# Two layernormed attention blocks on one Trainium2 core: inverse square roots as clamp and power on GpSimd, and a new order of the stages

## The chip, the cores and the metric

The kernel runs on one core of one Trainium2 chip. The metric is device time in microseconds for one execution; lower is better. The engines are named as the profile names them: PE (TensorE's matmuls), PEld (its weight loads), DVE (VectorE), ACT (ScalarE), POOL (GpSimd) and SP (SyncE, which issues most transfers).

## The reference

Eight sequences of 1024 tokens with 256 features pass first through a causal single-head attention with a residual and a layernorm (the first stage), then through a two-layer local transformer with 8 heads of 64 and a window of 128, then through a residual and a last layernorm. One local layer is, cut to what matters here:

```python
h = shift_token(x)                       # second half of the features moved by one token
q, k, v = split(h @ wqkv)
q = l2norm(q) * qs; k = l2norm(k) * ksc  # q / clip(||q||, 1e-12), head by head
q, k = rotary_xpos(q, k)
o = local_attention(q, k, v)             # each window of 128 sees itself and the one before
x = x + o @ wo
h = shift_token(x)
h = (h - mean(h)) / sqrt(var(h) + 1e-05) * lg + lb
a, g = split(h @ w1 + b1)
x = x + (a * gelu(g)) @ w2 + b2
```

Inverse square roots occur in three places: in `l2norm` (of the sum of squares of each head), in the layernorm ahead of the feed-forward part, and in the two outer layernorms.

## The kernel before, in words

The first stage (`fronts`) handles the eight sequences one after the other and writes its result to DRAM. Then `layers` walks over 2 layers x 8 sequences x 8 windows of 128 tokens, in 64 pairs of windows. Matrix products are done in split form: an operand is cut into a rounded high part and a remainder, and three products are added up.

The work on a window is cut into named stages. `prep` loads and transposes x for a pair. `qk` (twice a window, `k` 0 and 1) projects queries and keys of four heads (`l_pqk`), squares them on ACT (L705), sums the squares on DVE into `l_ss` (L708), multiplies the projections with the rotary tables on DVE (L715) and adds the two halves on POOL (L722). `unit` turns the sums of squares of a window, 16 numbers per token, into inverse norms `l_nrm` through `rsqrt`, and scales the keys with them on POOL (L733); the queries' norms are applied later, by the mask pass on the scores (L793). `turn` transposes queries and keys on PE (`l_t`, L756) and splits them into a ring of three windows. `sc` makes the scores of four heads, masks them on DVE (L793) and takes the exponential on ACT (`l_e`); `et` transposes the result (L832), `v` projects the values, `val` multiplies (`l_po`, L849), `out` divides by the denominators (L858, L863, L864), and `proj` projects back (`l_py`).

When the odd window of a pair is projected, the feed-forward part of the pair is put on a queue. It is a generator with eleven steps; the item `side` in the order runs the next step. The first step moves rows by one token with small transfers, takes mean and variance on DVE, calls `rsqrt` for 2 numbers per token (`m_rs`) and normalizes (`m_hn`, L917). The second transposes (`m_hp`) and splits. Six steps make the wide product and the gelu (`m_pag`, L965 to L970, whose last part on POOL is `m_a`), two the product back (`m_pf`), and the last adds the residual; in the second layer it also does the last layernorm, with an `rsqrt` of its own (`o_rs`). The first stage has a layernorm too (`f_rs`, 4 numbers per token, 16 calls).

The order of the stages is written out by hand in `ORDER`. For every pair `j` the list is run through once; an item `("sc", -2, 0)` means the scores of the heads' first half for window `2j - 2`. The instructions are written in that order, and the scheduler of the tile framework may move one ahead of another on its engine where its own model of the engines finds the earlier one not ready, so that the order on a chip is near the list, not the list itself. Each engine then takes its instructions in the order given. PSUM has four banks for the general tiles (`ps`) and four for scores (`sc`).

In `rsqrt`, the value is clamped or offset and scaled, its bits are read as an integer to make a first guess, and two refining steps follow: nine DVE instructions (L112 to L129).

Of the kernel before, what the change touches and what calls it, by code (L numbers as in the profile page):

```python
# [8 lines left out]

FP = mybir.dt.float32  # L10
FR = mybir.dt.float32r
I32 = mybir.dt.int32
AF = mybir.ActivationFunctionType
ALU = mybir.AluOpType
AX = mybir.AxisListType

P = 128
# [4 lines left out]
EPS = 1e-5  # L22
FAR = 1e30
BIG = 3e38
RS = (1595890143.0, 2.371616, -6.578563, 19.474865, 212.91114082351987)


@with_exitstack
def kernel(
# [31 lines left out]
    nc = tc.nc  # L61
# [22 lines left out]
    const = ctx.enter_context(tc.tile_pool(name="const", bufs=1))  # L84
# [20 lines left out]

    def rsqrt(sm, src, n, low, op, name):

        k, c1, c2, c3, f = RS  # L110
        a = sm([P, n], f"ra{n}", f"{name}_a", bufs=2)
        nc.vector.tensor_scalar(a, src, low, f, op, ALU.mult)  # L112
        seed = sm([P, n], f"ri{n}", f"{name}_i", bufs=2, dt=I32)
        nc.vector.tensor_scalar(seed, a.bitcast(I32), -0.5, k, ALU.mult, ALU.add)
        y = seed.bitcast(FP)
        t = sm([P, n], f"rt{n}", f"{name}_t", bufs=2)
        nc.vector.tensor_tensor(t, a, y, ALU.mult)
        u = sm([P, n], f"ru{n}", f"{name}_u", bufs=2)
        nc.vector.scalar_tensor_tensor(u, t, -1.0, y, ALU.mult, ALU.mult)
        z = sm([P, n], f"rz{n}", f"{name}_z", bufs=2)  # L120
        nc.vector.scalar_tensor_tensor(z, u, c1, y, ALU.add, ALU.mult)
        t = sm([P, n], f"rt{n}", f"{name}_t2", bufs=2)
        nc.vector.tensor_tensor(t, a, z, ALU.mult)
        h = sm([P, n], f"ru{n}", f"{name}_h", bufs=2)
        nc.vector.tensor_tensor(h, t, z, ALU.mult)  # L125
        p = sm([P, n], f"rp{n}", f"{name}_p", bufs=2)
        nc.vector.scalar_tensor_tensor(p, h, c2, h, ALU.add, ALU.mult)  # L127
        r = sm([P, n], f"ry{n}", f"{name}_y", bufs=6)
        nc.vector.scalar_tensor_tensor(r, p, c3, z, ALU.add, ALU.mult)  # L129
        return r  # L130

    def mean_rstd(sm, parts, mv, i, name):
# [7 lines left out]
    def rstd_of(sm, mv, n, name):  # L140
        return rsqrt(sm, mv[:, :, 1], n, EPS, ALU.add, name)


    ident = const.tile([P, P], FP, name="ident")
    make_identity(nc, ident)
    identr = const.tile([P, P], FR, name="identr")
# [5 lines left out]
    for j, s in ((0, 1), (1, -1), (2, 1)):  # L152
        nc.gpsimd.affine_select(
            out=mask[:, j, :], in_=mask[:, j, :], compare_op=ALU.is_ge, fill=FAR,
# [339 lines left out]
    def load_ffn(l, stage, ps, W):  # L494
# [90 lines left out]
    QB = 4  # L585
    PSB = {"ps": 4, "sc": 4}
    ORDER = [
        ("side", 1), ("out", -4), ("side", 1), ("side", 1), ("unit", -1), ("proj", -4),
        ("unit", -2), ("turn", -2, 0), ("turn", -1, 0), ("turn", -1, 1), ("sc", -2, 0),
        ("turn", -2, 1), ("qk", 0, 0), ("out", -3), ("side", 1), ("sc", -2, 1), ("side", 1),  # L590
        ("side", 1), ("proj", -3), ("sc", -1, 0), ("qk", 0, 1), ("v", 1), ("et", -2, 0),
        ("sc", -1, 1), ("et", -2, 1), ("v", 0), ("et", -1, 0), ("val", -2, 0), ("et", -1, 1),
        ("prep", 2), ("qk", 1, 0), ("side", 1), ("side", 1), ("qk", 1, 1), ("val", -1, 0),
        ("val", -2, 1), ("val", -1, 1), ("side", 1), ("side", 1), ("side", 1),
    ]

    def layers(pool, psum):
# [59 lines left out]
        def attention(l, b, W, finished):  # L657
# [67 lines left out]
            def unit(t):  # L725

                n = f"l{l}_{b}_{t}"
                nrm = rsqrt(sm, st.pop(("ss", t)), 2 * HEADS, 1e-24, ALU.max, f"{n}_nrm")
                st["nrm", t] = nrm
                n4 = nrm.rearrange("p (g k h) -> p g k h", g=2, k=2)  # L730
                for k in range(2):
                    kk = st["r", t, k][:, INNER // 2 :].rearrange("p (h d) -> p h d", d=DH)
                    nc.gpsimd.tensor_tensor(  # L733
                        kk, kk, n4[:, k, 1, :].unsqueeze(2).to_broadcast([P, HEADS // 2, DH]),
                        ALU.mult,
                    )
# [311 lines left out]
    with tc.tile_pool(name="fpool", bufs=1) as fpool, tc.tile_pool(  # L1048
        name="fpsum", bufs=1, space=PSUM
    ) as fpsum:  # L1050
        fronts(fpool, fpsum)
    with tc.tile_pool(name="lpool", bufs=1) as lpool, tc.tile_pool(
        name="lpsum", bufs=1, space=PSUM
# [59 lines left out]
```

## Time and profile before

| | us |
|---|---|
| median of three runs | 2795.12 |
| lowest and highest | 2794.61, 2795.77 |
| the profiled execution's own time | 2790.89 |
| its span, first to last instruction | 2789.1 |

The granted TensorE clock was 0.984 of full speed over the span. The page gives the busy time of each engine; groups of instructions by line, with busy time, mean duration and the idle time of the engine ahead of them; the chain that ended last, followed back from the last instruction to whatever released each step; and waits. PE's ends are modelled, so its busy share says that it has work in flight, not that it runs at its peak. Durations below come from the profiled execution.

### The profile page before, as it was taken

The page shows a single profiled execution, that of the slowest core. Times are in us where ns is not written, and L with a number is a line of the kernel's source. Part 1 is how long each engine was busy: PE and PEld are TensorE (multiplying, and loading weights), DVE is VectorE, ACT ScalarE, POOL GpSimd, SP SyncE. Part 2 cuts the span into 40 slices and gives each one's busy share as a digit, 9 for nine tenths or more (in the row PEclk, how much of TensorE's full clock was granted, in tenths as well). Part 3 has the DMA queues.
Part 4 walks back from the last instruction along what each step waited for, and adds up shares of the span by engine and source line. Part 5 has one row for each costly group of instructions (what it writes and reads, how often), then busy time and mean ns, then how long its engine had stood idle before and what let it go on. Part 6 is the DMA issues. An engine that isn't in the chain of part 4 may idle for free.

```text
span 2789.1 us, 63147 instructions
## 1 busy us (share of the span) xinstructions
PE 2703.2 (97%) x22336; PEld 2350.4 (84%) x22336; DVE 2440.2 (87%) x8464; ACT 1748.8 (63%) x4486; POOL 1245.9 (45%) x1515
## 2 busy tenths in 40 slices
PE   7998999999999999999999999999999999999997
PEld 5776688888888888888888788888888888888886
DVE  6887789888889988889888899999999999999995
ACT  6675566666666666666666566666666666666663
POOL 4553244444444444344453444444444454444442
PEclk9999899999999999999999999999999999999998
DMA  6332011011111111111111111111111111111110
GB/s 181 97 98 86 26 39 43 28 43 43 43 41 39 34 38 43 43 41 39 37 57 52 57 51 49 39 41 49 51 50 40 39 48 50 51 41 43 43 47 24
DMA packets 146126, 139.83 MB, mean 50 GB/s; under 512 B 28680, under 2 KB 122768, under 8 KB 145808
## 3 DMA queue, kind: packets, MB, share of 16 engines
q1 hardware_dynamic: 144448, 135.32, 16.0%
q8 instruction: 176, 2.88, 0.4%
q14 instruction: 142, 1.16, 0.1%
q10 hardware_dynamic: 1360, 0.46, 0.1%
HBM read 95.35 MB, written 27.81 MB: 44 GB/s over the span
## 4 chain that ended last, share of the span: by engine, by line
PE 69%; DVE 22%; ACT 3%; DMA 3%; issue 2%; POOL 0%; SPq 0%; DVEq 0%; POOLq 0%; ACTq 0%
PE l_pqk L104 11%; PE m_pag L104 9%; PE m_pf L104 9%; PE l_sc L785 8%; PE l_et L832 7%; PE l_po L849 6%; PE l_pv L104 5%; PE l_py L104 4%; PE l_t L756 3%; DVE l_t L715 3%; DVE m_gl L966 3%; DVE m_a L969 2%; DVE l_nrm_p L127 1%; DVE l_ss L708 1%; DVE l_sc L793 1%
## 5 line engine op out<-in xcount | busy, mean ns | idle before, releaser
L722 POOL TENSOR_TENSOR l_t<-l_t,l_t 128x256 f32<-128x256 f32 x512 | 367.5, 739 | 855.1 <-DVE l_t L715 816.0
L654 ACT ACTIVATE l_e<-l_sc,l_nm 128x256 f32<-128x256 f32 (+1 forms) x992 | 450.6, 462 | 288.4 <-DVE l_nm L793 279.3
L104 PE MATMUL m_pag<-m_hT,w_h 128*128 128x256 f32 (+1 forms) x2816 | 515.1, 285 | 6.4 <-DVE l_t L715 3.3
L793 DVE CUSTOM_DVE_ANT_0 l_sc<-l_sc,mask,l_nrm_y 128x256 f32<-128x256 f32 (+1 forms) x1024 | 453.6, 470 | 50.6 <-ACT l_e L654 36.0
L104 PEld LDWEIGHTS m_pag<-m_hT,w_h 128*128 128x128 f32 (+1 forms) x2816 | 430.3, 187 | 21.1 <-issue 10.5
L654 ACT ACTIVATE m_gl<-m_pag,b 128x256 f32<-128x256 f32 (+1 forms) x384 | 181.4, 474 | 385.2 <-PE m_pag L104 332.6
L104 PE MATMUL m_pag<-m_hT,w_l 128*128 128x256 f32 (+1 forms) x1408 | 393.7, 280 | 0.0
L104 PE MATMUL l_pqk<-wqk_h,l_xT 128*128 128x512 f32 x1024 | 392.4, 424 | 0.8 <-ACT l_xT L92 0.8
L715 DVE TENSOR_TENSOR l_t<-l_pqk,l_tab 128x512 f32<-128x512 f32 x512 | 329.8, 680 | 0.0
L835 ACT COPY l_eT<-l_et 128x512 f32<-128x512 f32 (+1 forms) x512 | 276.0, 567 | 80.6 <-PE l_et L832 56.3
L970 POOL TENSOR_TENSOR m_a<-m_gl,m_a 128x256 fp32r<-128x256 f32 x320 | 241.4, 762 | 113.2 <-DVE l_nrm_h L125 55.4
L832 PE MATMUL l_et<-ident,l_e 128*128 128x128 f32 x1920 | 269.9, 279 | 4.4 <-ACT l_eT L835 3.4
L104 PEld LDWEIGHTS m_pag<-m_hT,w_l 128*128 128x128 f32 (+1 forms) x1408 | 264.7, 188 | 0.0
L832 PEld LDWEIGHTS l_et<-ident,l_e 128*128 128x128 f32 x1920 | 215.2, 141 | 49.9 <-ACT l_eT L835 13.3
L104 PE MATMUL m_pf<-w_h,m_a 128*128 128x256 f32 x1280 | 249.5, 284 | 0.0
L849 PE MATMUL l_po<-l_eT,l_v 128*64 128x128 f32 x3840 | 242.0, 278 | 0.7 <-ACT l_eT L835 0.6
L104 PEld LDWEIGHTS l_pqk<-wqk_h,l_xT 128*128 128x128 f32 x1024 | 196.0, 191 | 53.9 <-ACT l_xT L92 1.2
L849 PEld LDWEIGHTS l_po<-l_eT,l_v 128*64 128x64 f32 x3840 | 209.5, 138 | 35.2 <-issue 18.8
L104 PEld LDWEIGHTS m_pf<-w_h,m_a 128*128 128x128 f32 x1280 | 203.5, 188 | 11.0 <-POOL m_a L970 0.2
L864 POOL TENSOR_TENSOR l_oT<-l_on,l_oT 128x512 fp32r<-128x512 f32 x128 | 165.0, 1289 | 97.5 <-ACT l_oT L863 92.6
L785 PE MATMUL l_sc<-ring,ring 64*128 64x256 f32 (+1 forms) x2048 | 207.5, 283 | 0.0
L104 PE MATMUL l_py<-wo_h,l_oT 128*128 128x256 f32 x1024 | 205.0, 282 | 0.0
(195 smaller groups left out, 6636.4 us busy)
## 6 DMA issues: line engine op xcount, KB each, us to landing
l_R<-rd_d SPq DMA_DIRECT2D x256, 128.0 KB
x<-x_d SPq DMA_DIRECT2D x96, 256.0 KB
l_tab<-tab_d SPq DMA_DIRECT2D x128, 128.0 KB
xin<-in_L_attn_x_dram SPq DMA_DIRECT2D x16, 512.0 KB
x_d<-xin SPq DMA_DIRECT2D x16, 512.0 KB
rd_d<-l_rT SPq DMA_DIRECT2D x512, 1.0 KB
x_d<-x SPq DMA_DIRECT2D x32, 256.0 KB
out_dram<-x SPq DMA_DIRECT2D x32, 256.0 KB
```

Source lines behind the costliest of these rows:

```text
L104: nc.tensor.matmul(dst, a, b, start=(i == 0), stop=(i == len(steps) - 1))
L654: ins = nc.scalar.activation(*args, **kw)
L715: nc.vector.tensor_tensor(tt[j].rearrange("p (k h d) -> p k h d", k=2, d=DH), p3, tb.unsqueeze(2).to_broadcast([P, 2, HEADS // 2, DH]), AL ...
L722: nc.gpsimd.tensor_add(a[:, :, s, :], a[:, :, s, :], bsw[:, :, 1 - s, :])
L756: nc.tensor.transpose(pt[:, cols], r[:, cols], ident)
L785: nc.tensor.matmul(sc[i][:, j, 0:nk], ring[x][rows, 0, c, slot, :], ring[y][rows, 1, c, keys, :], start=(m == 0), stop=(m == 2),)
L793: nc.vector.tensor_tensor_reduce(dst, dst, mk, st["nrm", w][:, 8 * u + h : 8 * u + h + 1], BIG, ALU.add, ALU.min, nm[:, one],)
L832: nc.tensor.transpose(pt[:, a, i, :], e[:, i, j, a * P : (a + 1) * P], ident)
L835: nc.scalar.copy(eT[:, j, 0:m], pt[:, 0:m])
L849: nc.tensor.matmul(po[i * DH : (i + 1) * DH, c * P : (c + 1) * P], st["v", t][:, head * DH : (head + 1) * DH], eT[:, j, a, i, :], start=(a ...
L864: nc.gpsimd.tensor_tensor(oT[1], on, oT[0].bitcast(FP), ALU.subtract)
L970: nc.gpsimd.tensor_tensor(a[1], gl[0:z, :], a[0].bitcast(FP), ALU.subtract)
```

## The change

Two edits are made together. `rsqrt` becomes two GpSimd instructions: clamp (or offset), then a power with a constant tile of -0.5, in place of the nine DVE instructions. And `ORDER` is replaced by another order of the same items: `unit` of the even window comes ahead of that of the odd one and farther from it, the turns are set apart by other work, the transposes of the scores of window -2 are done together, and the value products lie elsewhere. Buffers and everything else stay.

```diff
-RS = (1595890143.0, 2.371616, -6.578563, 19.474865, 212.91114082351987)
...
     def rsqrt(sm, src, n, low, op, name):
-        k, c1, c2, c3, f = RS
         a = sm([P, n], f"ra{n}", f"{name}_a", bufs=2)
-        nc.vector.tensor_scalar(a, src, low, f, op, ALU.mult)
-        seed = sm([P, n], f"ri{n}", f"{name}_i", bufs=2, dt=I32)
-        nc.vector.tensor_scalar(seed, a.bitcast(I32), -0.5, k, ALU.mult, ALU.add)
-        y = seed.bitcast(FP)
-        t = sm([P, n], f"rt{n}", f"{name}_t", bufs=2)
-        nc.vector.tensor_tensor(t, a, y, ALU.mult)
-        u = sm([P, n], f"ru{n}", f"{name}_u", bufs=2)
-        nc.vector.scalar_tensor_tensor(u, t, -1.0, y, ALU.mult, ALU.mult)
-        z = sm([P, n], f"rz{n}", f"{name}_z", bufs=2)
-        nc.vector.scalar_tensor_tensor(z, u, c1, y, ALU.add, ALU.mult)
-        t = sm([P, n], f"rt{n}", f"{name}_t2", bufs=2)
-        nc.vector.tensor_tensor(t, a, z, ALU.mult)
-        h = sm([P, n], f"ru{n}", f"{name}_h", bufs=2)
-        nc.vector.tensor_tensor(h, t, z, ALU.mult)
-        p = sm([P, n], f"rp{n}", f"{name}_p", bufs=2)
-        nc.vector.scalar_tensor_tensor(p, h, c2, h, ALU.add, ALU.mult)
+        nc.gpsimd.tensor_scalar(a, src, low, None, op)
         r = sm([P, n], f"ry{n}", f"{name}_y", bufs=6)
-        nc.vector.scalar_tensor_tensor(r, p, c3, z, ALU.add, ALU.mult)
+        nc.gpsimd.tensor_tensor(r, a, half.to_broadcast([P, n]), ALU.pow)
         return r
...
+    half = const.tile([P, 1], FP, name="half")
+    nc.gpsimd.memset(half, -0.5)
...
     ORDER = [
-        ("side", 1), ("out", -4), ("side", 1), ("side", 1), ("unit", -1), ("proj", -4),
-        ("unit", -2), ("turn", -2, 0), ("turn", -1, 0), ("turn", -1, 1), ("sc", -2, 0),
-        ("turn", -2, 1), ("qk", 0, 0), ("out", -3), ("side", 1), ("sc", -2, 1), ("side", 1),
-        ("side", 1), ("proj", -3), ("sc", -1, 0), ("qk", 0, 1), ("v", 1), ("et", -2, 0),
-        ("sc", -1, 1), ("et", -2, 1), ("v", 0), ("et", -1, 0), ("val", -2, 0), ("et", -1, 1),
-        ("prep", 2), ("qk", 1, 0), ("side", 1), ("side", 1), ("qk", 1, 1), ("val", -1, 0),
-        ("val", -2, 1), ("val", -1, 1), ("side", 1), ("side", 1), ("side", 1),
+        ("side", 1), ("unit", -2), ("out", -4), ("side", 1), ("proj", -4), ("turn", -2, 0),
+        ("unit", -1), ("turn", -2, 1), ("side", 1), ("turn", -1, 0), ("sc", -2, 0),
+        ("turn", -1, 1), ("sc", -2, 1), ("side", 1), ("qk", 0, 0), ("side", 1), ("out", -3),
+        ("qk", 0, 1), ("side", 1), ("proj", -3), ("sc", -1, 0), ("et", -2, 1), ("et", -2, 0),
+        ("v", 1), ("side", 1), ("v", 0), ("et", -1, 0), ("val", -2, 0), ("prep", 2),
+        ("sc", -1, 1), ("side", 1), ("qk", 1, 0), ("et", -1, 1), ("val", -2, 1), ("qk", 1, 1),
+        ("val", -1, 0), ("val", -1, 1), ("side", 1), ("side", 1), ("side", 1),
     ]
```

More of the change, by code (lines that the diff above doesn't have):

```diff
@@ L11 @@
 FR = mybir.dt.float32r
-I32 = mybir.dt.int32
 AF = mybir.ActivationFunctionType
```

## The prediction

> **What bounds the kernel now.** I read the page first: which engine is full, and whether it is full everywhere.
>
> ```profile
> PE 2703.2 (97%) x22336; PEld 2350.4 (84%) x22336; DVE 2440.2 (87%) x8464; ACT 1748.8 (63%) x4486; POOL 1245.9 (45%) x1515
> ```
>
> TensorE's bar is full, but its ends are modelled, so I went to the chain that ended last, through one pair of windows of layer 0, from one group of `l_xp` transposes to the next.
>
> ```profile
> 908.32 0.44 PE l_xp L677 x4
> 908.75 1.53 PE l_pqk L104 x6
> 910.28 0.44 PE m_hp L931 x4
> 910.72 1.39 PE l_pqk L104 x6
> 912.10 1.90 PE l_po L849 x32
> 914.00 8.01 PE m_pag L104 x66
> 922.01 1.43 PE l_py L104 x12
> 923.44 2.01 PE l_t L756 x16
> 925.45 1.11 PE l_sc L785 x12
> ...
> 945.53 1.02 PE l_et L832 x8
> 946.56 0.48 PE l_xp L677 x4
> ```
>
> Columns: start, length, what. All of it is TensorE, each run beginning where the last ended: 946.56 - 908.32 = 38.24 us a pair, 64 pairs, some 2400 us of the 2789.1. Six score matmuls and the like run at their own pace; only `l_t`, 2.01 us for 16 transposes where four of `l_xp` take 0.44 (16 would take 1.76), shows waiting. So the vector work that the change removes lies beside TensorE here. Is that so in layer 1? Two stretches of four pairs (one sequence), the first of layer 0, the second of layer 1, side by side in the table by windows; the columns are PE, PEld, DVE, ACT, POOL busy.
>
> ```profile
> 412.20:563.50 151.30, 151.15 (x1287) 133.72 (x1286) 134.57 (x449) 97.74 (x248) 66.24 (x86) 1.00 0.13 40
> 1685.00:1839.30 154.30, 153.11 (x1291) 134.64 (x1290) 142.32 (x510) 98.05 (x248) 71.30 (x89) 1.00 0.15 46
> ```
>
> TensorE issues the same matmuls, yet layer 1 takes 3.0 us more, with DVE at 142.32 of 154.30. The chain inside that second stretch tells why:
>
> ```profile
> 1783.70 0.74 DVE l_nrm_u L119
> 1784.64 0.40 DVE m_gl L966
> 1785.58 0.68 DVE l_nrm_p L127
> ...
> 1788.22 0.67 DVE l_nrm_y L129
> 1788.88 0.41 DVE m_gl L966
> ...
> 1790.89 0.66 PE l_t L756 x4
> ```
>
> Here the pieces of `rsqrt` stand between TensorE's runs: DVE sets the end for some 9 us in one pair of four. That is where the change can pay.
>
> **The removed instructions.** Nine on DVE for each call, 240 calls: 128 in `unit` on 16 columns, 64 + 32 on 2, 16 on 4. In the groups by shape the nine `l_nrm` rows are busy 73.2 + 51.0 + 45.6 + 41.0 + 29.9 + 26.1 + 23.9 + 23.3 + 22.4 = 336 us (2.6 us a call), the nine `m_rs` rows 92, `o_rs` 65, `f_rs` some 25: 518 us, 21% of DVE. Some of it is waiting:
>
> ```profile
> L127 DVE SCALAR_TENSOR_TENSOR l_nrm_p<-l_nrm_h x128: 161/660/733, 280.4 to 2713.3; 128x16 f32<-128x16 f32 x128
> ```
>
> Minimum, median and maximum in ns: 161 when free, mostly as long as one GpSimd operation (606 to 735 ns median). The Trainium skill, "GPSIMD Engine Reference", section 8, says that the two engines share SBUF interfaces and collide where the vector instruction has two SBUF inputs; by it about 9 x 0.16 = 1.5 us of a call is work and the rest waiting, and both end alike.
>
> Priced on the path, not by the 518 us: (a) layer 0 and 1, each pair: the waits in `l_t` go, 2.01 - 1.76 = 0.25 us. (b) layer 1's excess, 3.0 us x 8 sequences = 24 us: I take two thirds, -16, since score and transpose runs are also cut finer there, which the change need not mend. (c) between the layers (1450 to 1460, 1490 to 1502, 1533 to 1541) and near 2710 the same `l_nrm` pieces are on the chain: four places at 2 us, -8. Bounds for (b) and (c): 0 and -24, 0 and -15. In the first stage 16 calls of nine pieces at some 0.17 us lie among 260 us that wait on many things: within 3 us either way, taken as nothing.
>
> **The added instructions.** A clamp and a power on GpSimd. No row shows a power. Below: GpSimd's plain products cost 739 ns for 256 columns and 1289 for 512, so 2.15 ns a column and 0.19 us fixed; 16 columns make 0.22 us, and that is the clamp. Above: the nine-piece DVE chain, 2.7 us, as another iterated way to the same function. I take 2.0 us (nine GpSimd passes of 0.22 us), nearer the upper end because the work is alike; 2 columns, 0.5 us. The same skill page, section 7, charges a dependent fp32 chain 4 cycles an element at 1.2 GHz; a chain of 30 steps would be an estimated 1.6 us for 16 columns, and the sum would not move.
>
> Where does it lie? Per pair GpSimd is busy 17.95 of 38.24 us; 2 x 2.2 + 0.7 (0.7 more in layer 1) makes some 23. The tight stretch runs from the second `l_pqk` of a pair to the first `m_pf`, in the new order 1.90 (values) + 7.28 (60 of the 66 `m_pag`) + 1.43 + 0.88 + 0.73 + 0.44 + 0.91 + 0.44 + 0.91 = 14.9 us. `l_ss` is there 2.0 us in (912.10 to 914.14 in the timeline), so 12.9 us are left, and in them stand
>
> ```profile
> L722 POOL TENSOR_TENSOR l_t<-l_t,l_t 128x256 f32<-128x256 f32 x512 | 367.5, 739 | 855.1 <-DVE l_t L715 816.0
> L970 POOL TENSOR_TENSOR m_a<-m_gl,m_a 128x256 fp32r<-128x256 f32 x320 | 241.4, 762 | 113.2 <-DVE l_nrm_h L125 55.4
> L864 POOL TENSOR_TENSOR l_oT<-l_on,l_oT 128x512 fp32r<-128x512 f32 x128 | 165.0, 1289 | 97.5 <-ACT l_oT L863 92.6
> ```
>
> 2 x 0.74 + 6 x 0.76 + 1.29 and four of L733 at 0.65 = 9.9 us: 3.0 us left. One unit's 2.2 us fits; the other's sums of squares are ready half a pair earlier, where GpSimd idles over 3 us at a time (816.0 us in all, the first row's last column). Cost on the path: nothing, while clamp and power stay under 3.0 us and the first unit is early. The new wait is GpSimd's for `l_ss`; queued behind it are L722, L970 and L864, and TensorE waits for those in `l_t`, `m_pf`, `l_py`. DVE's mask pass L793 and `m_hn` now wait for GpSimd.
>
> **The new order.** Eleven feed-forward steps a pair as before, exps and gelus alternate twice a pair as before. By runs of TensorE: the turns stand apart (saving counted in a); a value run of 32 (1.90) becomes 16 and 16 (1.05 each in the layer 1 chain) and the transposes behind such a run take 1.02 for 0.87: +0.35; 16 `l_et` together, -0.15; two fewer `l_pqk` runs straight behind scores (1.59 for 1.39), two transposes there instead: -0.1; a split `m_pag` +0.1. With (a) about -0.1 a pair (bounds -0.35 to +0.3): -6 us over 64.
>
> From `l_py` of the odd window to `m_hp` there are now 8.9 us of TensorE runs (12 before). The timeline has 10.1 us from that `l_py`'s end (934.67) to the last `m_hn` (944.72), of which `rsqrt` is 940.39 to 943.56: 6.9 us are left and 0.7 of GpSimd, so 1.3 us spare if GpSimd is free, as it is there (3.3 us idle before L921). SP's transfers move with their stages (shifted rows with the first feed-forward step, reciprocals with the scores, x with `prep`); the table loads have no producer to wait for, so I price that at nothing; if it is uncovered, a landing of some 3 us in a pair would show. For small new waits I put 0.1 us a pair, +6.
>
> **Sum.** -6 - 16 - 8 + 6 = -24 us on the profiled execution's 2790.9 (span 2789.1 and 1.8 around it): 2767. The median of the three runs, 2795.1, is 4.2 above it: 2771.
>
> **Rivals.** (1) No change: TensorE is full, DVE was covered, the new order gives back what layer 1 gains. For it: layer 0's chain. Against: the layer 1 chain. 2795 within 5. (2) Slower: the power is dear. From 3.0 us for clamp and power (or if both units fall in the tight stretch) every further us delays `m_pf` or `l_t` each pair; at 4.25 us 1.25 x 64 = 80, less 24: 2851. Against: GpSimd's half-empty pair. For: its 3 us of room there. (3) Slower: 16 `l_et` fill four PSUM banks just behind the scores, ACT (24.73 us of 38.24, dense there) runs four exps at 0.68 us (475 + 203 ns) before it can empty the second bank, and `l_pv` waits up to 1.3 us. Above 0.4 us a pair it outweighs the gain; at the full 1.3, 83 less 24: 2854. Against: before, ACT was as dense and TensorE did not wait. (4) The order alone undone by more runs, +0.3 a pair: +19 - 24, same as (1).
>
> **Chances.** Forecast 0.48; no change (1, 4) 0.10; (2) 0.20; (3) 0.22. A difference of 0.2%, 5.6 us, is about what a measurement of this kernel can tell. Low end: (a) to (c) at their gaining bounds, -0.35 x 64 - 24 - 15 = -61, not all at once: 2742. High end: near the full price of (2) or (3), 2850; dearer cases are left out. The forecast's own range is 2742 to 2789.
>
> **What would show it.** Right: DVE near 1920 us; layer 1's four pairs under 152 us; no `l_nrm` piece on the chain; `l_t` waiting on nothing long; clamp and power under 3 us. Wrong: POOL over 70%, TensorE idle before `l_t` or `m_pf` with a GpSimd releaser (2), or before `l_pv` with an ACT one (3).

## The result and the profile after

The change makes the kernel slower: a median of 2912.41 us (2906.86 to 2918.93) against 2795.44, a ratio of 1.042 (95% interval 1.0394 to 1.0446). The profiled execution took 2908.46 us, 117.6 more than the one before. I split both spans at the copies of the first transposes of each pair (`l_xT <- l_xp` in ACT's timeline, 64 of them):

| us | before | after | difference |
|---|---|---|---|
| up to the first pair | 262.8 | 264.3 | +1.6 |
| 32 pairs of layer 0 | 1180.3 | 1154.8 | -25.6 |
| layer 1, up to its last pair | 1220.1 | 1367.0 | +146.9 |
| the rest | 125.9 | 120.6 | -5.3 |

Layer 0 and the end gain; layer 1 loses nearly 5 us a pair. The engine totals show that it isn't work that grew on TensorE's side (page of the kernel after):

```profile
PE 2697.8 (93%) x22336; PEld 2382.4 (82%) x22336; DVE 2133.7 (73%) x6304; ACT 1743.3 (60%) x4486; POOL 1734.5 (60%) x1996
```

DVE is 306 us lighter, POOL 489 heavier and still at 60%, while PE's share fell from 97% to 93%. The table by windows of the kernel after, over four pairs of layer 0 and four of layer 1 (columns PE, PEld, DVE, ACT, POOL busy, granted clock, DMA share, GB/s), puts the loss in layer 1, with a lower granted clock beside it, 0.92:

```profile
1040.35:1190.75 150.40, 148.44 (x1290) 133.60 (x1289) 117.05 (x341) 96.81 (x249) 93.94 (x109) 1.00 0.13 40
2207.89:2385.15 177.26, 158.18 (x1288) 141.34 (x1289) 123.83 (x364) 98.44 (x248) 102.32 (x122) 0.92 0.14 40
```

In layer 0 the chain through a pair is TensorE alone, as before, and 37.57 us long from one `l_xp` to the next instead of 38.24; the transposes of queries and keys wait for nothing now (`l_t` x8 in 0.87, where 16 took 2.01):

```profile
1079.42 0.59 PE l_xp L659 x4
...
1086.08 7.29 PE m_pag L102 x60
1093.36 1.40 PE l_py L102 x12
1094.76 0.87 PE l_t L738 x8
...
1116.99 0.58 PE l_xp L659 x4
```

The chain of layer 1, between two pairs, is a different one:

```profile
2111.31 0.23 POOL o_rs_a L107
2111.54 1.15 POOL l_t L715 x2
2112.68 0.69 POOL o_rs_y L109
...
2113.40 0.73 DVE x L979 x2
...
2114.16 2.16 DMA out_dram<-x
...
2116.38 2.75 DMA x<-x_d
2119.26 1.09 PE l_xp L659 x4
2120.35 0.85 PE m_hp L913 x4
2121.20 2.56 PE l_pqk L102 x6
```

The end of one pair's last layernorm releases the store of its output, the store's end releases a load of `x`, and that load is what `prep`'s transposes wait for. The waits of PE sum it up (total in us, times, longest): one wait of 4.7 us before the change; after it 130.8 us, 28 times, every pair of layer 1 but the first few.

```profile
PE l_xp L677 <- DMA x<-x_d: 4.7, 1, 4.7
PE l_xp L659 <- DMA x<-x_d: 130.8, 28, 7.6
```

Why must a load wait for a store? The tiles of `prep`'s x and of x0, which the feed-forward part of layer 1 adds, are drawn from one set of five buffers (`load_x`, tag `x`), and a load starts when its buffer is free. SP's timeline shows who got which buffer. Before the change:

```profile
2002.61 0.41 SPq L626 DMA_DIRECT2D out_dram<-x  x1
2004.84 0.37 SPq L621 DMA_DIRECT2D x<-x_d  x1
...
2010.02 0.54 SPq L621 DMA_DIRECT2D x<-x_d  x1
```

and after:

```profile
2114.16 0.41 SPq L608 DMA_DIRECT2D out_dram<-x  x1
...
2116.38 0.39 SPq L603 DMA_DIRECT2D x<-x_d  x1
...
2118.04 0.38 SPq L603 DMA_DIRECT2D x<-x_d  x1
```

Each time one load follows the store at once and the other comes later. Before, the first is x0, whose addition on POOL runs from 2008.55 to 2009.84; that frees its buffer for `prep`'s x, loaded from 2010.02 on and transposed only at 2044.72, 35 us later. In the new order the feed-forward step that asks for x0 stands ahead of `prep` in the list, and the two swap: the first load (2116.38) is `prep`'s, transposed at 2119.26 as soon as it lands, and x0 (2118.04) lies unused for 43 us, until its addition at 2161.18. The lines for these uses (POOL and PE before, POOL after):

```profile
2008.55 1.29 POOL L925 TENSOR_TENSOR x<-x,x 128x512 f32<-128x512 f32 x1
2044.72 0.64 PE L677 MATMUL l_xp<-ident,x 128*128 128x128 f32 x4
2161.18 1.26 POOL L907 TENSOR_TENSOR x<-x,x 128x512 f32<-128x512 f32 x1
```

In layer 0 there is no x0, and no such wait.

The second cost comes through the clock. The table by windows around that stop:

```profile
2117.00:2118.00 1.00, 0.00 (x0) 0.00 (x0) 0.00 (x0) 0.00 (x0) 1.00 (x2) 0.81 0.43 71
2118.00:2119.20 1.20, 0.00 (x0) 0.00 (x0) 0.00 (x0) 0.00 (x0) 1.20 (x2) 0.50 0.52 171
2119.20:2123.20 4.00, 3.94 (x14) 3.48 (x15) 1.50 (x4) 1.17 (x2) 0.03 (x1) 0.50 0.44 129
2123.20:2124.20 1.00, 1.00 (x6) 0.80 (x5) 0.00 (x0) 0.40 (x1) 0.00 (x0) 0.50 0.00 0
2124.20:2125.20 1.00, 1.00 (x8) 0.95 (x8) 0.77 (x2) 0.77 (x3) 0.00 (x0) 0.88 0.00 0
```

TensorE is idle for 4.05 us, from 2115.2 to 2119.26. About 2.4 us into it the granted clock falls to 0.50 (the mean of 0.81 from 2117 to 2118 puts it at 2117.6), and it stays there until about 2124.4, through the first 5.2 us of work: `l_xp` takes 1.09 for 0.44, `m_hp` 0.85 for 0.44, `l_pqk` 2.56 for about 1.4: 2.2 us more for this stop.

Last, the operation that no row of before showed. POOL's groups by shape of the kernel after (instructions, busy us, mean ns, idle before):

```profile
L109 POOL TENSOR_TENSOR l_nrm_y<-l_nrm_a,half 128x16 f32<-128x16 f32 x128 | 374.0, 2922 | 10.6
L109 POOL TENSOR_TENSOR m_rs_y<-m_rs_a,half 128x2 f32<-128x2 f32 x64 | 47.0, 734 | 5.2
L107 POOL TENSOR_SCALAR l_nrm_a<-l_ss 128x16 f32<-128x16 f32 x128 | 32.4, 253 | 26.7 <-DVE l_ss L690 21.4
```

A power of 16 columns takes 2.92 us, not 2.0; with the clamp 3.18. Yet no wait of PE for POOL ranks among the long ones.

### The profile page after: what moved, and what is told of

Its sections match the earlier page's. It is cut to its first block, busy times and chain, and to the rows that moved or that the text cites. A ratio compares the mean times of both kernels' runs of the same rounds, so it can differ in the third digit from the quotient of the medians.

```text
span 2906.7 us, 61751 instructions
## 1 busy us (share of the span) xinstructions
PE 2697.8 (93%) x22336; PEld 2382.4 (82%) x22336; DVE 2133.7 (73%) x6304; ACT 1743.3 (60%) x4486; POOL 1734.5 (60%) x1996
## 4 chain that ended last, share of the span: by engine, by line
PE 63%; ACT 12%; DVE 12%; DMA 8%; POOL 3%; issue 2%; SPq 0%; POOLq 0%; DVEq 0%; ACTq 0%
PE m_pag L102 17%; PE l_pqk L102 10%; ACT l_e L636 7%; PE l_po L831 6%; PE l_et L814 4%; PE l_sc L767 4%; PE l_py L102 4%; PE l_t L738 4%; DVE l_t L697 3%; PE m_pf L102 3%; DMA x<-x_d 3%; PE l_pv L102 2%; DMA out_dram<-x 2%; ACT L636 2%; PE l_xp L659 2%
## 5 line engine op out<-in xcount | busy, mean ns | idle before, releaser
L775 DVE CUSTOM_DVE_ANT_0 l_sc<-l_sc,mask,l_nrm_y 128x256 f32<-128x256 f32 (+1 forms) x1024 | 434.5, 465 | 63.2 <-ACT l_e L636 45.7
L102 PE MATMUL l_pqk<-wqk_h,l_xT 128*128 128x512 f32 x1024 | 401.2, 434 | 0.8 <-ACT l_xT L90 0.8
L109 POOL TENSOR_TENSOR l_nrm_y<-l_nrm_a,half 128x16 f32<-128x16 f32 x128 | 374.0, 2922 | 10.6
L948 DVE SCALAR_TENSOR_TENSOR m_gl<-m_pag,b,m_gl 128x256 f32<-128x256 f32 (+1 forms) x384 | 184.4, 480 | 167.0 <-ACT m_gl L636 165.2
L687 ACT ACTIVATE l_sq<-l_pqk 128x512 f32<-128x512 f32 x256 | 155.2, 606 | 222.4 <-PE l_pqk L102 222.3
L814 PE MATMUL l_et<-ident,l_e 128*128 128x128 f32 x1920 | 276.6, 285 | 7.6 <-ACT l_e L636 4.9
L814 PEld LDWEIGHTS l_et<-ident,l_e 128*128 128x128 f32 x1920 | 227.7, 147 | 53.5 <-ACT l_e L636 11.5
L102 PEld LDWEIGHTS l_pqk<-wqk_h,l_xT 128*128 128x128 f32 x1024 | 209.3, 204 | 42.4 <-ACT l_xT L90 1.2
L690 DVE TENSOR_REDUCE l_ss<-l_sq 128x8 f32<-128x512 f32 x256 | 174.6, 682 | 91.9 <-ACT l_sq L687 89.3
```

What stands on the lines that cost most here:

```text
L102: nc.tensor.matmul(dst, a, b, start=(i == 0), stop=(i == len(steps) - 1))
L109: nc.gpsimd.tensor_tensor(r, a, half.to_broadcast([P, n]), ALU.pow)
L690: nc.vector.tensor_reduce(st["ss", t][:, k * HEADS : (k + 1) * HEADS], sq.rearrange("p (g d) -> p g d", d=DH), AX.X, ALU.add)
L775: nc.vector.tensor_tensor_reduce(dst, dst, mk, st["nrm", w][:, 8 * u + h : 8 * u + h + 1], BIG, ALU.add, ALU.min, nm[:, one],)
L814: nc.tensor.transpose(pt[:, a, i, :], e[:, i, j, a * P : (a + 1) * P], ident)
L948: nc.vector.scalar_tensor_tensor(gl[0:z, :], a_ps, W["b1"][0:z, 0, m : m + 1], gl[0:z, :], ALU.add, ALU.mult)
```

## The experiments

My theory after this look: the slowdown is the order of two items, the request for x0 and `prep`, through shared buffers, and has nothing to do with the power; without it the change gains. The rivals: the dear power (the forecast's second rival), the order by itself in other ways, and the store's time.

**Each part alone.** First the power in the old order:

```diff
 (the new rsqrt)
-    ORDER = (the new list)
+    ORDER = (the list of the kernel before)
```

> The clamp and power on GpSimd, with the order of the stages as before. Theory A (the new order makes prep's load of x wait for the store of the last output, in layer 1 alone; the power is not the cause): no TensorE wait for x from DRAM, four pairs of layer 1 near 150 to 156 us, in all 2760 to 2810 us. Theory B (the power, 2.9 us for 16 columns, is too dear for GpSimd's queue): slower than before by 60 us or more, TensorE waiting before l_t or m_pf with GpSimd's l_t or m_a as the releaser.

Measured: 2925.33 us, ratio 1.0478 (1.046 to 1.0495). As slow as the whole change, but elsewhere: 71.2 us more than before in layer 0, 62.0 in layer 1, some 2.1 us in every pair. Its POOL timeline shows both units' powers back to back, and the halves of `l_t` behind them:

```profile
957.54 0.47 POOL L107 TENSOR_SCALAR l_nrm_a<-l_ss 128x16 f32<-128x16 f32 x2
957.96 5.79 POOL L109 TENSOR_TENSOR l_nrm_y<-l_nrm_a,half 128x16 f32<-128x16 f32 x2
963.70 1.43 POOL L704 TENSOR_TENSOR l_t<-l_t,l_t 128x256 f32<-128x256 f32 x2
```

The amount is that of theory B, but its sign is not: PE waits in `l_t` mostly for DVE's work on the gelus and on x, and only 3 times (16.0 us) for POOL's `l_t`. The waits of PE, and of ACT, in this run:

```profile
PE l_t L738 <- DVE m_gl L948: 56.6, 129, 2.6
PE l_t L738 <- DVE x L861: 32.0, 62, 0.5
ACT l_oT L845 <- PE l_py L102: 264.9, 63, 4.5
```

ACT now stands at `l_oT` with the pair's last three gelus behind it; in the kernel before it waits there 34.7 us in all, and the gelus stand ahead of it. So the power in the old order costs 131 us, by a path that the profile leads through DVE and ACT; how much of it is POOL's lateness and how much the changed order of ACT's instructions is not shown here. A run below moves one of the two units. Then the nine vector instructions in the new order:

```diff
 (the new ORDER)
-    rsqrt as clamp and power
+    rsqrt as the nine DVE instructions
```

> The nine vector instructions as before, with the new order of the stages. Theory A: the layer 1 stall stays, since it comes from the order: l_xp waits for x in nearly every pair of layer 1, four pairs there take 170 us or more, in all 2880 to 2960 us. Theory B: no such stall, 2780 to 2810 us. If the GpSimd queue ahead of the last layernorm (3.6 us in the chain) is a good part of the stall, four pairs of layer 1 take 165 or less.

Measured: 2989.16 us, ratio 1.0708 (1.0692 to 1.0724), somewhat above theory A's range. The wait for the load is there without any power, and larger than in the kernel after:

```profile
PE l_xp L677 <- DMA x<-x_d: 168.5, 29, 7.8
PE m_hp L931 <- DVE m_hn L917: 28.1, 15, 5.9
```

The order makes it, then; and there is a second wait in it, for the normalized rows `m_hn`.

**Which two items.** `prep` is moved ahead of the feed-forward step that asks for x0, the rest of the change stays:

```diff
-        ("v", 1), ("side", 1), ("v", 0), ("et", -1, 0), ("val", -2, 0), ("prep", 2),
+        ("v", 1), ("prep", 2), ("side", 1), ("v", 0), ("et", -1, 0), ("val", -2, 0),
```

> The change with one item moved: prep ahead of the feed-forward step that loads x0 for the last residual, so that x is given its buffer first. Theory A: x takes the buffer that the add of x0 gave back a pair earlier, x0 the one that the store gives back; the wait of l_xp for DRAM goes, layer 1's four pairs fall from 177 to 150 to 154 us, in all 2750 to 2775 us. Theory B: the wait was only the last link of a late GpSimd chain; another one takes its place, still over 2850 us.

Measured: 2800.25 us, ratio 1.0032 (1.0017 to 1.0047), between the two theories' ranges. `l_xp` no longer waits for a load and layer 1 falls from 1367.0 to 1224.6 us. But the early `prep` has a price of its own: its work on x^T now stands ahead of other work in DVE's queue, and the value products wait behind it, and layer 0 rises from 1154.8 to 1187.7.

```profile
PE l_po L831 <- DVE l_cx L666: 53.4, 44, 6.9
```

**Buffers.** x0 gets a buffer of its own and x keeps four, five in all:

```diff
-            "sh": 3, "a": 10, "gl": 3, "x": 5, "tab": 2,
+            "sh": 3, "a": 10, "gl": 3, "x": 4, "x0": 1, "tab": 2,
...
-            t = tl("x", [P, 2, E], f"{name}_{b}_{p}")
+            t = tl("x0" if name == "x0" else "x", [P, 2, E], f"{name}_{b}_{p}")
```

> The change with x0 in a buffer of its own and four buffers for x in place of five shared by both; the order is the new one. Theory A: x's load then always needs the store's buffer, as there are three x in flight and the fourth: the wait for the store stays or grows, over 2880 us, and now layer 0 waits for its store too; it shows that the buffer count and not the place in the list decides. If layer 0 is slower than 150.4 us for four pairs, that is the sign.

Measured: 2914.38 us, ratio 1.0439 (1.0416 to 1.0463), no different from the kernel after. Store, load and transposes still follow one another:

```profile
PE l_xp L659 <- DMA x<-x_d: 134.2, 29, 6.5
```

With four buffers for x alone, `prep`'s x has none but the one that the store gives back. So the five are enough only as long as x0 is the one that takes the late buffer; a sixth wasn't tried. The expected sign in layer 0 did not show: it took 1157.7 us, hardly more than the 1154.8 of the kernel after.

**The request behind prep.** The load of x0 and its addition are moved from the first feed-forward step to the start of the second, which in the new order stands behind `prep`. No stage moves:

```diff
-            x0 = load_x(b, p, x0_d, "x0") if last_layer else None
...
-            if x0 is not None:
-                nc.gpsimd.tensor_add(x1, x1, x0)
             yield
+            if last_layer:
+                x0 = load_x(b, p, x0_d, "x0")
+                nc.gpsimd.tensor_add(x1, x1, x0)
```

> The change, with x0 for the last residual loaded and added one feed-forward step later, behind prep in the list; the order of the stages stays. Theory A (x and x0 share five buffers; in the new order x0 is asked for first and takes the one that came free a pair earlier, so prep's x waits for the store): l_xp waits for DRAM no more, layer 1's pairs fall from 44 to 38 us, in all 2912 - 32 x 6 = 2720, 2705 to 2745 us, faster than before. Theory B (GpSimd's late last layernorm is the root, the buffer its symptom): layer 1's pairs stay over 41 us, as another wait for GpSimd comes up; over 2800 us.

Measured: 2733.11 us (2724.36 to 2738.77), ratio 0.9787 (0.9759 to 0.9816). That is 179 us less than the change as it was made, and better than both kernels. The edit moves x0's addition on POOL as well as its load; the run with `prep` first, which left the addition where it was, lost the wait too, so the wait hangs on the order of the two loads. Layer 1 takes 1189.7 us, 30.4 less than before the change; layer 0 1152.6, 27.7 less. Of the long wait one is left, as in the kernel before, and PE is full again (page, then the waits of PE):

```profile
PE 2639.5 (97%) x22336; PEld 2329.3 (86%) x22336; DVE 2125.5 (78%) x6304; ACT 1729.8 (64%) x4486; POOL 1735.4 (64%) x1996
```

```profile
PE l_xp L659 <- DMA x<-x_d: 4.7, 1, 4.7
```

The same edit made to the kernel before, as a control:

> A control: the kernel before with x0 loaded and added one step later. In the old order prep already stands ahead of x0. If x0 later is a gain of its own and not the removal of the new order's stall, this falls by 50 us or more; by theory A it stays within 15 us of the kernel before.

Measured: 2792.37 us, ratio 0.9992 (0.9981 to 1.0002). It does nothing there, so the 179 us are the stall of the new order and not a gain of the edit in itself.

**The same stall, made in the kernel before.** Nine DVE instructions, the old order, with one feed-forward step moved ahead of `prep`:

```diff
-        ("prep", 2), ("qk", 1, 0), ("side", 1), ("side", 1), ("qk", 1, 1), ("val", -1, 0),
+        ("side", 1), ("prep", 2), ("qk", 1, 0), ("side", 1), ("qk", 1, 1), ("val", -1, 0),
```

> The kernel before with one item moved: the feed-forward step that loads x0 stands ahead of prep. Theory A: the stall appears in the old order too, with no power in the kernel: l_xp waits for x from DRAM in nearly every pair of layer 1, layer 0 unchanged at 151.3 us for four pairs, +100 to +220 us. Theory B: no change beyond 20 us.

Measured: 2845.76 us, ratio 1.0197 (1.0163 to 1.0231), some 55 us more. Layer 0 is unchanged (1179.6 us), layer 1 is 53.9 us longer. The sign and the place are as expected, the size isn't: only 12 pairs wait for the load, and less long; the rest is put down to ACT.

```profile
PE l_xp L677 <- DMA x<-x_d: 30.4, 12, 4.8
PE l_xp L677 <- ACT l_eT L835: 23.2, 17, 1.6
```

**Power and order without the stall.** With x0 asked for later, the nine DVE instructions in the new order:

```diff
 (new ORDER, x0 behind prep)
-    rsqrt as clamp and power
+    rsqrt as the nine DVE instructions
```

> The nine vector instructions with the new order and the later x0. Says what clamp and power are worth when the stall is gone. Theory A: the new order is what gains in layer 0 and the power only must not stand in the way: layer 0's pairs near 38 us, in all 2740 to 2790 us, 15 to 50 us above the kernel with clamp and power. Theory B (the power costs even in the new order): this one is the faster of the two.

Measured: 2864.08 us, ratio 1.0258 (1.0234 to 1.0281): the power is worth 131 us in this order, far more than the 15 to 50 expected. The longest of the new waits, about half of the loss, is that for the layernorm, whose nine pieces no longer fit between `l_py` and `m_hp`:

```profile
PE m_hp L931 <- DVE m_hn L916: 66.4, 29, 5.9
```

Next, the nine instructions in the layernorms alone, the power in `unit`:

```diff
-        return rsqrt(sm, mv[:, :, 1], n, EPS, ALU.add, name)
+        return rsqrt_nine(sm, mv[:, :, 1], n, EPS, ALU.add, name)
```

> The kernel with the later x0 and the new order, clamp and power for the units' 16 columns alone; the layernorms' 2 to 4 columns by the nine vector instructions. If the new order's short way from l_py to m_hp needs the layernorm's short power (0.22 + 0.73 us for nine vector instructions spread over 3 us), m_hp waits for m_hn and it is slower than the 2733 us of the kernel with the later x0 by 30 us or more; if the units' relief of DVE is what counts, it is within 15 us of it.

Measured: 2787.76 us, ratio 0.9981 (0.9969 to 0.9993), 55 us above the version with both powers. So of the 131 us about 55 hang on the power in the layernorms, the rest on that in `unit`.

```profile
PE m_hp L941 <- DVE m_hn L926: 37.3, 12, 5.9
```

And in the old order, with the even window's unit moved right behind its own `qk`, half a pair earlier:

```diff
-        ("unit", -2), ("turn", -2, 0), ...
+        ("turn", -2, 0), ...
...
-        ("qk", 0, 1), ("v", 1), ...
+        ("qk", 0, 1), ("unit", 0), ("v", 1), ...
```

> Clamp and power in the old order, with the unit of the even window placed straight behind its projections, half a pair earlier. If the old order with powers is slow because both powers (5.8 us) stand one behind the other ahead of the second window's halves and keys, this takes most of its 131 us away: 2780 to 2830 us, and l_t's wait goes. If the power is too dear wherever it stands, it stays over 2890 us.

Measured: 2806.41 us, ratio 1.0046 (1.0031 to 1.0061). One item takes back 119 of the 131 us that the power cost in the old order; the two powers of a pair now lie apart, `l_t` is off the list of long waits, and ACT's wait at `l_oT` is down to 29.9 us. The longest wait of PE that is left is that of `l_sc` for the ring's split, 0.7 us each time; next is `m_pag` for DVE's `l_t`, 19.0 us in all:

```profile
PE l_sc L767 <- DVE ring L91: 32.5, 46, 0.8
```

**How much cover there is.** On the best version, every power is issued twice, the first result unused:

```diff
+        w = sm([P, n], f"rw{n}", f"{name}_w", bufs=2)
+        nc.gpsimd.tensor_tensor(w, a, half.to_broadcast([P, n]), ALU.pow)
         r = sm([P, n], f"ry{n}", f"{name}_y", bufs=6)
         nc.gpsimd.tensor_tensor(r, a, half.to_broadcast([P, n]), ALU.pow)
```

> The kernel with the later x0, and each power run twice (the first result is not used): 2.9 us more of GpSimd for each unit. If the new order really hides the power (the first unit runs in GpSimd's idle time), a second one of 5.8 us a pair costs less than 2 us a pair, under 2850 us. If clamp and power already fill the stretch from the second l_pqk to m_pf, each further us of power comes on top: 64 x 4 to 64 x 6, over 2950 us.

Measured: 3048.55 us, ratio 1.0917 (1.0892 to 1.0943), 315 us above the same kernel with one power. POOL's busy time rises by 439 us, so seven tenths of the doubled work lands on the end. It comes out as a wait for the feed-forward part's norm rather than for `l_t`:

```profile
PE m_hp L915 <- DVE m_hn L900: 171.1, 45, 6.1
```

## Why the prediction was wrong

I forecast 2771 us and a gain; it was a loss of 4.2%, above the range's end of 2850.

**The step that failed** is the sentence on SP's queue: that its transfers, "x with `prep`" among them, move with their stages, and that the table loads have no producer to wait for, "so I price that at nothing". The load of x got no price of its own. I thought of the producers of a transfer's data and not of its destination. The load of x does have something to wait for: the buffer it writes. What was needed could be seen before: in the diff, a feed-forward step that comes to stand ahead of `prep`; in `load_x`, that both draw on tag `x`; and in SP's timeline of before, that `prep`'s load takes the buffer that x0 has just given back. The sign that I named for it, a landing of some 3 us in a pair, did show (2.75 us in the chain above), but its price is a whole chain, store and load and a cold clock: nearly 6 us a pair, 179 us in all (2912.4 less 2733.1).

**The rest of the sum**, read from the version in which only that wait is gone: 2733 instead of 2771, a gain of 66.5 us between the profiled executions (57 between the medians measured side by side) where I had 24.

- (a) and the order, -6 with a gaining bound of -22: too small. Layer 0 gains 27.7 us. Of that 11.8 lie in the first three intervals, where the pipeline fills (79.6 us before, 67.8 in this version), and the rest in the steady pairs: four usual ones take 148.4 us instead of 151.4, and a few of them are longer.
- (b) and (c): layer 1 gains 30.4 us and the end 7.5, where I had -16 and -8. No piece of DVE's `l_nrm` is left on the chain, as forecast; four usual pairs of layer 1 take about 151 us, under the 152 that I named.
- The new waits, +6, came to little: PE's waits inside the two layers add up to some 32 us, where the kernel before had 30.
- DVE near 1920 us was a wrong reading of rows: the nine pieces' rows sum to 516 us, but DVE fell by 306. The durations of DVE's instructions overlap: in the kernel before they add up to 3004 us where DVE is busy for 2440, and without the nine pieces the others still cover 2099, so that only 341 us were the pieces' alone. Part was also given back: the `m_a` cast takes a mean of 461 ns for 304.

**The power's price** was mis-sized: 2.92 us for 16 columns against 2.0 with a bound of 2.7, and clamp plus power 3.18 where I allowed 3.0. On the path it shows no price all the same: in the version without the stall PE waits for POOL 2.7 us in all. The assumption next to it was right: the even window's power falls into POOL's idle time, as the timeline of POOL after shows (the square bracket is idle time before the instruction):

```profile
1067.67 1.43 POOL L704 TENSOR_TENSOR l_t<-l_t,l_t 128x256 f32<-128x256 f32 x2 [7.33 <-DVE l_t L697]
1069.07 0.25 POOL L107 TENSOR_SCALAR l_nrm_a<-l_ss 128x16 f32<-128x16 f32 x1
1069.40 2.92 POOL L109 TENSOR_TENSOR l_nrm_y<-l_nrm_a,half 128x16 f32<-128x16 f32 x1
```

**The rivals.** The second, the dear power with both units in the tight stretch, is real, but in the old order: there it costs 131 us, on a path that is not settled, and moving one unit takes nearly all of it back. Its price per us fits in part: with every power doubled, layer 0 gets 98.5 us longer, 3.1 us a pair for 2.92 more in the tight stretch, but layer 1 192.3 us, 6.2 a pair, and the wait comes before `m_hp`, not before `l_t` or `m_pf`. What it wasn't is the cause of this result. The third, `l_pv` behind four exps, is next to nothing in every run (0.2 us, once, in the one with `prep` first). The room from `l_py` to `m_hp` held: with the power that path waits for `m_hn` twice, 5.2 us in all; with nine DVE instructions it overflows by up to 6 us in a pair.

Order and power thus need each other: the old order loses 131 us by taking the power, and the new one, with x0 asked for later, would lose 131 us by giving it up.

## What to carry to other kernels

When an order of stages changes, list for each queue not only what a transfer reads but what its destination waits for: which buffers rotate under the same tag, who takes them first in the new order, and which of the takers can afford the late one. If one load of two must follow a store, let it be the one whose consumer is farthest from the critical engine. And a slow operation on a half-idle engine is priced by where its instances stand relative to one another, not by the engine's share.

## What the runs showed of the hardware

- A stop of TensorE cost more than its length here, as the granted clock was halved (0.50) for a while. In the stop shown above it fell 2.4 us after the work ended, and 5.2 us of work passed until it rose. Neither is a fixed delay: in the profile's record of the kernel after, the clock changes only at points of one raster of 3.41 us, and of 37 low stretches 27 last two of these periods, 7 one and 2 three. Over the 28 stops of layer 1 the fall comes 2.0 to 5.4 us after the work ended, at one of the raster's points. Two of the stops, whose work had ended at 2159.66 and 2201.96, in the table by windows (the clock is the third number from the end):

```profile
2161.99:2168.82 6.83, 4.74 (x17) 4.08 (x18) 1.55 (x4) 1.38 (x3) 1.68 (x2) 0.50 0.39 116
2206.36:2213.19 6.83, 5.30 (x19) 4.64 (x20) 1.67 (x5) 1.77 (x3) 1.49 (x2) 0.50 0.32 111
```

  The Trainium skill, "TensorE: Matmul & The Clock Gate", section "What's actually happening", puts the fall after an idle window of about 3.4 us, one that runs freely, and the recovery after a busy one. The length and the free running agree with this trace. The window need not be idle from end to end: the one before the fall at 2117.6 had 2.4 us of idle time. 28 stops of 4.7 us in the mean, with 2.2 us of slow work behind each, would be 193 us, a little more than the 177.3 us (5.7 a pair) that layer 1 loses against the version without the stall.
- GpSimd's power costs by the column: 734 ns for 2, 1023 for 4, 2922 for 16, so about 156 ns a column ((2922 - 734) / 14) and 0.42 us fixed, some 70 times its plain product (2.15 ns a column in the rows of before).
